# A tile's scatter stands two steps later in GpSimd's queue, in a four-layer graph attention kernel

## The chip, the cores and the metric

One Trainium2 chip, one core. The metric is the device time of one execution in microseconds (us).

## The reference

Four graph attention layers follow each other on 3327 nodes with 512 features, with 8, 4, 1 and 8 heads. Each layer normalizes, projects, scores every edge, takes a softmax over the neighbours and adds the weighted rows to `x`; layers 1 and 2 end in an ELU. Layer 0, with what all share:

```python
h = jnp.maximum(_layernorm(x, axis=-1), 0.0)
h = (h @ W.T).reshape(n, Hh, d)
e_src = jnp.einsum('nhd,hd->nh', h, a_src)
e_dst = jnp.einsum('nhd,hd->nh', h, a_dst)
e = jax.nn.leaky_relu(e_src[:, None, :] + e_dst[None, :, :], negative_slope=0.2)
mask = adj + jnp.eye(n, dtype=adj.dtype) > 0
e = jnp.where(mask[:, :, None], e, -jnp.inf)
alpha = jax.nn.softmax(e, axis=1)
out = jnp.einsum('ijh,jhd->ihd', alpha, h)
x = x + out.reshape(n, Hh * d)
```

The adjacency is sparse: a node has some 17 neighbours, itself included.

## The kernel before

A first part (to about 280 us of the profile) turns the rows of `adj` into neighbour lists and sorts the nodes by their degree into 26 tiles of 128. It also projects `x` for layer 0 into a table in DRAM, `tabx`. For layers 1 to 3 the tables are `tab`, two of them in turn. A row of a table has 528 numbers: the 512 projected features and the scores of the heads.

The second part, `tile_gat_lists`, runs the layers. Per layer it goes through the tiles from the one with the shortest lists to the one with the longest (11 to 36 slots, `CAPS`). The slots of a tile are cut into groups of four, and each group is a step, so that a tile takes 3 to 9 steps. A step of a group does this:

- `fetch`: GpSimd issues one indirect DMA per slot (L786), which gathers 128 rows of the table into a quarter of a buffer `g`. There are seven buffers `g` (`LOOK = 7`), and a step fetches the group that comes six steps later, so a fetch waits until VectorE has finished the group that used the buffer before.
- `scored`: VectorE adds the scores of source and target (`z`, L839, L841), ScalarE takes the exponential into `pw` (L842). It is done one step ahead of the products.
- `group`: with more than one head, VectorE multiplies the gathered rows by their weights into `m` (L865; three buffers), and TensorE adds the four products up in PSUM with matmuls by the identity (L870, tile `bank`). With one head VectorE does it alone (L860).

After a tile's last group at step `s` its end is spread over later steps: divisors and means on VectorE, the addition to `x` (`added`), and, except in the last layer, the next layer's normalization and projection: ScalarE subtracts the mean and squares (`xn` L915, `waste` L918), VectorE takes the root (`ve` L923 and on), TensorE transposes (`pt` L451), ScalarE applies the ReLU (`hT` L458), TensorE projects (`pv` L469), and ScalarE scales the result into the block of rows `v` (L476, three buffers). Then SP copies `v` to `own` (L941), and GpSimd scatters `v` into the next layer's table by an indirect DMA (L794), since the tiles are sorted and the table is not. In the last layer nothing is projected; the scatter there writes `x` to the output.

The order of the instructions is written out by hand: within the schedule TensorE, VectorE, ScalarE and GpSimd execute what is given to them in the order of the Python calls, whatever is ready. `later(s, place, piece)` puts a piece into step `s`; a step runs the fetch of the group six steps on, then the pieces at "first", the scores of the next group, the pieces at "scored", the products of this group, and the pieces at "last". A piece of one step on one engine thus stands in front of all pieces of later steps on that engine. `scatter` issues all scatters that wait at that moment. For a tile with more than one head `ends` is called with the step two after its last group.

Beside the lists, in layer 0 nine tiles of `adj` are gathered as masks (`Mask`), and in layers 1 to 3 the tiles with the longest lists (1, 9 and 2 of them) are computed densely with masks, in pieces between the same steps (`Several`, `Wholes`); these end through `ends` as well.

Of the kernel before, what the change touches and what calls it, by code (L numbers as in the profile page):

```python
# [22 lines left out]
HEADS = [8, 4, 1, 8]  # L23
# [724 lines left out]
def tile_gat_lists(ctx: ExitStack, tc: tile.TileContext, x, adj, ws, avs, out, ident, half, slots, L, low, spare, tabx, tabs):  # L748
# [48 lines left out]
    class Tile:  # L797
# [146 lines left out]
        def ends(self, s):  # L944

            b = s + 1 if ELU[self.l] else s
            for d, place, piece in [(s + 1, "scored", self.bent), (b, "last", self.added),
                                    (b + 1, "scored", self.centre), (b + 1, "last", self.root),
                                    (b + 2, "first", self.turn), (b + 2, "last", self.cut),
                                    (b + 3, "last", self.project), (b + 5 - (HEADS[self.l] == 1), "scored", self.rows),  # L950
                                    (b + 5, "last", scatter)]:
                later(d, place, piece)

        def finish(self, s):
# [319 lines left out]
    def later(s, place, piece):  # L1274
        at.setdefault((s, place), []).append(piece)
# [120 lines left out]
```

## Time and profile before

| what | us |
|---|---|
| median of three runs | 2964.49 |
| lowest, highest of them | 2949.65, 2972.24 |
| the profiled execution: time | 2978.08 |
| the profiled execution: span of its instructions | 2976.4 |
| first to last gather of layers 0, 1, 2, 3 in it (about) | 280 to 1072, 1112 to 1776, 1827 to 2275, 2318 to 2947 |
| busy: TensorE, VectorE, GpSimd, ScalarE | 2249.4, 1939.2, 1771.0, 890.3 |

The profile is of one execution. Engines are PE (TensorE), DVE (VectorE), ACT (ScalarE), POOL (GpSimd) and SP. A group's row gives the line, the engine, the operation, what is written and read, the count, then the busy time and the mean of one in ns, then the idle time of the engine just ahead of these instructions and what ended it. In a timeline each row has its start, its duration, and in brackets the idle time ahead of it and who ended it; "issue" is time in which the engine waited for nothing that the profile shows, "remote" a release whose origin it does not show.

### The profile page before, as it was taken

How to read it: one execution, taken by the hardware profiler on the slowest of the kernel's cores; microseconds unless marked ns; L12 is line 12 of the kernel's file. 1: busy time of each engine (PE TensorE's matmuls, PEld its weight loads, DVE VectorE, ACT ScalarE, POOL GpSimd, SP SyncE). 2: the span in 40 equal slices, each digit the busy share in tenths (PEclk: the TensorE clock that was granted, in tenths of full speed). 3: DMA queues.
4: the chain of work that ended last, by engine and by line, in shares of the span. 5: the costliest groups of instructions: out<-in, count | busy, mean ns of one | idle time of the engine just before them, and what ended most of it. 6: DMA issues, size and time to landing. Idle time of an engine off the chain costs nothing. (4 is left out here: it accounts for less than half of the span.)

```text
span 2976.4 us, 26618 instructions
## 1 busy us (share of the span) xinstructions
PE 2249.4 (76%) x6832; PEld 1233.1 (41%) x6832; DVE 1939.2 (65%) x5056; ACT 890.3 (30%) x2321; POOL 1771.0 (60%) x1774
## 2 busy tenths in 40 slices
PE   3777687777866775789787776768795588887877
PEld 2665243433433332445344433335454344444443
DVE  8897656645644545677566664787888366666656
ACT  4782122222211112333223222343333232323221
POOL 6993565655655636566566653565554566666664
PEclk9888888988988897999898988889798788888889
DMA  6784577776776657767676754777775666666664
GB/s 234 289 322 153 164 235 228 229 220 206 233 216 185 184 129 206 207 208 222 188 215 203 213 167 147 234 228 250 215 253 160 179 202 200 197 200 194 197 197 127
DMA packets 253306, 612.96 MB, mean 206 GB/s; under 512 B 90963, under 2 KB 108371, under 8 KB 248662
## 3 DMA queue, kind: packets, MB, share of 16 engines
q0 software_dynamic: 131120, 455.33, 51.6%
q1 hardware_dynamic: 118278, 149.01, 15.4%
q10 hardware_dynamic: 3744, 6.82, 0.7%
q8 instruction: 56, 0.92, 0.1%
q14 instruction: 108, 0.88, 0.1%
HBM read 544.13 MB, written 66.89 MB: 205 GB/s over the span
## 5 line engine op out<-in xcount | busy, mean ns | idle before, releaser
L870 PE MATMUL bank<-m,ident 128*128 128x512 f32 x2608 | 1320.9, 655 | 322.3 <-DVE m L865 189.4
L865 DVE TENSOR_TENSOR m<-g,pw 128x512 f32<-128x512 f32 x1304 | 810.9, 681 | 535.3 <-ACT pw L842 309.4
L870 PEld LDWEIGHTS bank<-m,ident 128*128 128x128 f32 x2608 | 525.9, 209 | 973.8 <-issue 631.1
L786 POOL DMA_INDIRECT g<-tab,idxb x734 | 701.7, 956 | 376.5 <-issue 199.8
L469 PE MATMUL pv<-w,hT 128*128 128x264 f32 x1664 | 450.7, 429 | 82.3 <-ACT hT L458 42.4
L469 PEld LDWEIGHTS pv<-w,hT 128*128 128x128 f32 x1664 | 349.9, 213 | 189.2 <-ACT hT L458 48.9
L786 POOL DMA_INDIRECT g<-tabx,twiceb x342 | 324.9, 950 | 148.6 <-issue 94.8
L786 POOL DMA_INDIRECT g<-tab,idxa x297 | 285.2, 960 | 159.6 <-issue 85.9
L842 ACT ACTIVATE pw<-z 128x32 f32<-128x32 f32 (+5 forms) x434 | 83.3, 192 | 878.1 <-DVE z L841 454.4
L1069 PE MATMUL whole<-ve,em 128*128 128x512 f32 x468 | 229.5, 639 | 52.5 <-DVE em L1055 17.3
L794 POOL DMA_INDIRECT tab<-v,idxb x54 | 54.1, 1002 | 243.6 <-ACT v L476 219.7
L630 POOL TENSOR_TENSOR key<-a,keys 128x3328 int32<-128x3328 int32 x26 | 189.4, 7293 | 4.2 <-DMA a<-in_adj 3.6
L860 DVE SCALAR_TENSOR_TENSOR bank<-g,pw,bank 128x512 f32<-128x512 f32 x243 | 183.2, 754 | 12.5 <-DVE bank L860 3.2
L1069 PEld LDWEIGHTS whole<-ve,em 128*128 128x128 f32 x468 | 92.0, 203 | 167.1 <-issue 114.3
L451 PE MATMUL pt<-ident,xn 128*128 128x128 f32 x416 | 70.8, 297 | 107.8 <-ACT xn L915 25.6
L637 DVE MAX8 cand<-key 128x8 f32<-128x208 int32 x416 | 143.6, 364 | 1.4 <-POOL key L630 1.4
L839 DVE TENSOR_TENSOR z<-g,pw 128x32 f32<-128x32 f32 (+5 forms) x434 | 74.3, 171 | 102.8 <-DMA g<-tab,idxa 63.0
L786 POOL DMA_INDIRECT g<-tabx,twicea x99 | 94.7, 957 | 74.9 <-issue 41.5
L458 ACT ACTIVATE hT<-pt 128x512 f32<-128x512 f32 x104 | 61.1, 588 | 200.0 <-remote 111.6
L476 ACT ACTIVATE v<-pv,rstd 128x528 f32<-128x528 f32 x78 | 54.2, 695 | 210.7 <-PE bank L870 104.5
L451 PEld LDWEIGHTS pt<-ident,xn 128*128 128x128 f32 x416 | 53.6, 151 | 150.7 <-issue 48.6
L1210 ACT ACTIVATE spare<-room,low 128x64 f32<-128x64 f32 x208 | 57.8, 336 | 183.8 <-remote 81.7
(173 smaller groups left out, 2216.1 us busy)
## 6 DMA issues: line engine op xcount, KB each, us to landing
a<-in_adj SPq DMA_DIRECT2D x26, 1664.0 KB
own<-v SPq DMA_DIRECT2D x78, 264.0 KB
ve<-tab SPq DMA_DIRECT2D x78, 264.0 KB
g<-own SPq DMA_DIRECT2D x66, 264.0 KB
tabx<-vx SPq DMA_DIRECT2D x26, 528.0 KB
g<-tab,idxb POOLq DMA_INDIRECT x734
low<-tab SPq DMA_DIRECT2D x52, 132.0 KB
room<-tab SPq DMA_DIRECT2D x52, 132.0 KB
```

Of the source, the lines that this page charges most:

```text
L451: nc.tensor.transpose(pt[:, k, :], xn[:, k * P:(k + 1) * P], ident)
L458: nc.scalar.activation(hT, pt, AF.Relu)
L469: nc.tensor.matmul(pv[:, s, :HF + 8], hT[:, k, :], W.w[:, k, s, :], start=(k == 0), stop=(k == KC - 1))
L630: nc.gpsimd.tensor_tensor(key, a, keys, OP.mult)
L637: nc.vector.max(cand[:, g * 8:(g + 1) * 8], key[:, g * SEG:(g + 1) * SEG])
L786: nc.gpsimd.indirect_dma_start(out=out_, out_offset=None, in_=table, in_offset=bass.IndirectOffsetOnAxis(ap=which, axis=0))
L839: nc.vector.tensor_tensor(z, g[:, :n, ROW - 8:ROW - 8 + H], self.s.unsqueeze(1).to_broadcast([P, n, H]), OP.add)
L842: nc.scalar.activation(self.wt[:, k0:k0 + n, :H], z, AF.Exp)
L860: nc.vector.scalar_tensor_tensor(acc, v, w, acc, OP.mult, OP.add)
L865: nc.vector.tensor_tensor(m[:, q, :].rearrange("p (s h d) -> p s h d", s=2, d=D), v.rearrange("p s (h d) -> p s h d", d=D), wt[:, k0 + q, ...
L870: nc.tensor.matmul(self.po, ident, m[:, q, :], start=(k0 + q == 0), stop=(k0 + q == K - 1))
L1069: nc.tensor.matmul(tl.po.rearrange("p (s m) -> p s m", s=2), e[:, q * P:(q + 1) * P], v.rearrange("p (s m) -> p s m", s=2)[:, :, :F // 2], ...
```

## The change

In `ends`, the scatter of a tile is put at the end of step `b + 7` where it was at the end of `b + 5`, where the layer has more than one head (layers 0, 1 and 3). `rows`, which makes `v`, stays in step `b + 5`. For one head (layer 2) the expression gives `b + 5` as before.

```diff
                                     (b + 3, "last", self.project), (b + 5 - (HEADS[self.l] == 1), "scored", self.rows),
-                                    (b + 5, "last", scatter)]:
+                                    (b + 7 - 2 * (HEADS[self.l] == 1), "last", scatter)]:
                 later(d, place, piece)
```

In GpSimd's queue the scatters of layers 0, 1 and 3 move behind the gathers of two further steps. The orders of the other engines and of SP are the same as before. In layer 0, for example, a scatter that stood between 12 and 8 gathers now follows the 8.

## Prediction

> **What bounds the kernel now.** I read the page first, then the busy times by layer, then who waits for whom in each layer, then the scatter's own line, and last the timelines of GpSimd, ScalarE and VectorE around single scatters.
>
> ```profile
> PE 2249.4 (76%) x6832; PEld 1233.1 (41%) x6832; DVE 1939.2 (65%) x5056; ACT 890.3 (30%) x2321; POOL 1771.0 (60%) x1774
> ...
> L786 POOL DMA_INDIRECT g<-tab,idxb x734 | 701.7, 956 | 376.5 <-issue 199.8
> ...
> L794 POOL DMA_INDIRECT tab<-v,idxb x54 | 54.1, 1002 | 243.6 <-ACT v L476 219.7
> ```
>
> No engine is full over the span. GpSimd's 60% is misleading: in a run of gathers each takes 0.95 us and 0.30 us of issue, so one starts every 1.254 us. The second and third lines are the gathers and the scatters; the scatter's idle column is what the change is about: GpSimd stood 219.7 us waiting for the row block `v` that ScalarE writes at L476 (the `idxb` tiles alone).
>
> By layer (windows from each layer's first gather to its last):
>
> ```profile
> 280.00:1072.00 792.00, 591.93 (x1653) 295.85 (x1652) 450.91 (x1207) 157.14 (x325) 473.47 (x497) 0.87 0.70 209
> 1112.00:1776.00 664.00, 521.86 (x1476) 273.87 (x1477) 421.63 (x1135) 190.87 (x590) 406.91 (x428) 0.89 0.70 205
> ...
> 2318.00:2947.00 629.00, 499.56 (x1607) 264.71 (x1608) 381.42 (x802) 180.17 (x628) 386.07 (x403) 0.85 0.68 197
> ```
>
> The columns are length, PE, PEld, DVE, ACT, POOL busy with counts, clock, DMA share, GB/s. With 0.3 us added to each, GpSimd's 428 instructions in layer 1 take 428 x 1.254 = 537 of 664 us, in layer 0 623 of 792, in layer 3 505 of 629. The rest is pauses. In all three layers the period of a tile is thus GpSimd's issue time plus its pauses; TensorE's busy time (522 in layer 1) is almost as long. So both are candidates for the bound, and the question is what ends a pause.
>
> Now the waits of GpSimd at the scatter (us, times), of VectorE for gathered rows (us, times, longest), both in the window of layer 1:
>
> ```profile
>   ACT v L476: 95.2, 21
> DVE z L839 <- DMA g<-tab,idxa: 24.3, 6, 17.0
> ```
>
> In layer 0 the first is 122.9 us in 20 waits. But the second line says that the gathers held up behind the scatter are not late: VectorE waits for rows six times in layer 1, all at its start. In the timelines the last gather of a group is issued 11 to 36 us before VectorE takes the group, in the body of either layer. So GpSimd's wait as such costs nobody a late row.
>
> The last view is one scatter of layer 1, in the timelines of GpSimd, ScalarE and VectorE:
>
> ```profile
> 1349.86 0.95 POOL L786 DMA_INDIRECT g<-tab,idxb  x1 [0.30 <-issue]
> 1353.65 0.70 ACT L476 ACTIVATE v<-pv,rstd 128x528 f32<-128x528 f32 x1 [6.49 <-PE bank L870]
> 1354.63 0.99 POOL L794 DMA_INDIRECT tab<-v,idxa  x1 [3.82 <-ACT v L476]
> 1355.75 0.15 DVE L923 TENSOR_SCALAR ve<-squares 128x1 f32<-128x1 f32 x1 [6.08 <-ACT waste L918]
> 1355.92 0.97 POOL L786 DMA_INDIRECT g<-tab,idxb  x1 [0.30 <-DVE ve L923]
> ```
>
> TensorE had issued the last of `pv`'s matmuls at 1346.83, yet ScalarE gets word only at 1353.65, 2.84 us after GpSimd's last gather ended (1350.81). The same in layer 0, with `hT` at the head of ScalarE's queue:
>
> ```profile
> 694.38 0.94 POOL L786 DMA_INDIRECT g<-tabx,twiceb  x1 [0.30 <-issue]
> 706.86 0.99 POOL L794 DMA_INDIRECT tab<-v,idxb  x1 [11.54 <-ACT v L476]
> ...
> 698.68 0.60 ACT L458 ACTIVATE hT<-pt 128x512 f32<-128x512 f32 x1 [16.37 <-remote]
> ```
>
> `hT`'s transposes started at 682.09 to 682.41; ScalarE sees them at 698.68, 3.36 us after the last gather's end (695.32). Wherever ScalarE stands for a result of TensorE that is long done, the wait ends 2 to 4 us into a pause of GpSimd. In layer 3, which has no `v`, the pauses come from full gather buffers, and they are longer:
>
> ```profile
> 2684.76 0.95 POOL L786 DMA_INDIRECT g<-tab,idxb  x1 [0.30 <-issue]
> 2692.81 0.95 POOL L786 DMA_INDIRECT g<-tab,idxb  x1 [7.09 <-DVE m L865]
> ```
>
> My reading, inferred from the timing and not shown by a cause in the trace: while gathers stream, TensorE's signals are held back, and a pause lets them through. The scatter's wait is then a valve: it stops the stream once per tile, just when ScalarE needs TensorE's word.
>
> **What the skill says.** "Trainium Architecture — The Big Picture", section "Inside one NeuronCore": every engine has its own instruction stream and meets the others only through semaphores. The trace agrees: gathers whose buffer is free stand behind a scatter that waits (1355.92 follows 1354.63). "Perfetto Trace Analysis", section "DMA Instruction — SWDGE (GPSIMD)": the profiled end of such a DMA is the end of descriptor generation, not of the data. Agrees: the first group of layer 1 is issued by 1115.25 and used at 1118.00, 2.75 us later. "DMA: Bandwidth & Descriptors", section "Anatomy of one DMA — SWDGE (gpsimd) path", gives 2.0 us plus bytes over 436e3; for 264 KB that is an estimate of 2.6 us, near that 2.75, and near the time into a pause at which the held signals arrive. No page says that gathers hold TensorE's signals back.
>
> **The change part by part.** Nothing is removed or added: 26 scatters in each of layers 0, 1 and 3 move two steps later, past the gathers of two steps (up to 8, so 10 us of issue). SP's copy of `v` (L941) stays where it is. Layer 2 has one head and is unchanged.
>
> Layer 3: its scatter waits for the finished `x`, and nearly always goes at once; its three longest waits sum to 24.5 us, and no gather behind it is needed within 11 us. 0 us, at most 24 gained if that is wrong.
>
> Buffers: `v` has three, a tile lasts about 27 us, so a buffer is asked for again some 80 us later; holding it 10 us longer costs 0. Without that cover ScalarE would wait up to 10 us a tile. Ends of layers: the last gathers have been issued before the last scatters, so nothing is passed: 0.
>
> Layers 0 and 1, the scatter passed by gathers. For each scatter I looked up when VectorE had freed the buffer that the next step's gathers need. In layer 1, 16 scatters that waited over 1 us had it free by the start of the pause (within 0.3 us); 55 gathers stand there. In layer 0 it is 11 scatters and 45 gathers. At these 27 GpSimd will go on instead of pausing: 100 gathers x 1.254 = 125 us of streaming before the valve opens, if signals come only in pauses. The buffer after that is typically free 9 us after the old pause began, and VectorE's way there leads through ScalarE's blocked `v`, so the pause comes anyway, later, and ends only when VectorE has finished another group. After the release in the example VectorE needs `ve`, the root (2 us), divisors, `z`, and four products (2.48 us), to 1361.70: 8 us, against the 1 us that the scatter needed.
>
> What a pause becomes: the 27 last 3.7 us on average now. Ended by a buffer, layer 3 shows what they last: 23 over 3 us sum to 132, so 5.7 us. Upper bound, with the longer way of layer 1: a delay of the whole 125 us, and 20 more for buffers that come free later. I take layer 3's value, measured, because some signals do pass during a stream: 27 x (5.7 - 3.7) = +54 us. At nine further scatters of layer 0 the buffer comes free only after the pause began; GpSimd then resumes at the buffer instead of at `v`; their sum is -9 us. Total +45 us. Lower bound: every wait at a scatter in layers 0 and 1 (218 us) is pure loss; see the rivals.
>
> **The sum.** The profiled execution spans 2976.4 and took 2978.1 us; +45 gives 3023. The median shown is 2964.5, 13.6 lower, so 3010 us there, 1.5% slower.
>
> **Rivals.**
> First, a wash: the rows are early, GpSimd's wait turns into a wait for buffers of the same length. For it: layer 3 without any such wait pauses about 5.2 us a tile, layer 1 4.9, layer 0 6.2. Layer 1 would gain 0.3 a tile, layer 0 lose 1.0: +7 - 25 = -18 us, about 2946, no measurable difference. Against it: the chain from ScalarE to the next free buffer is longer in layers 0 and 1 than in layer 3.
> Second, the other side: the blocked queue is the loss, as it looks. GpSimd issues for 537 of 664 us in layer 1; if its pauses there and in layer 0 (127 and 169 us) shrink by about a fifth, since a stream that starts earlier gives VectorE and TensorE deeper stock, the gain is 60 us: 2905. It decides if TensorE's signals are late for another reason than the stream (then the release does not wait for a pause, and a pause is only lost issue time). For it: GpSimd's issue time is the longest sum in layer 0. Against it: no row is late.
> Third, signals held throughout: +145 us, 3110, if nothing passes during a stream.
> That the change does nothing: no, the order in GpSimd's queue differs in layers 0, 1 and 3.
>
> **How the numbers follow.** Slower by the later valve 0.45, held throughout 0.10, wash 0.20, faster 0.25. A measurement of this kernel tells about 1% from no change. So slower 0.55, same 0.20, faster 0.25. The range 2900 to 3090 takes in the wash and the faster case at its value, and the slower case up to 125 us; beyond are the held-throughout case and larger gains. The likeliest case alone runs from 2985 to 3050.
>
> **What would show it.** Right: the wait of the scatter for `v` in layers 0 and 1 falls from 218 us to under 40; GpSimd's waits for VectorE's buffers rise by more than that; the waits of `hT` and `v` on TensorE grow; layer 2 keeps its length and layer 3 too; layers 0 and 1 together grow by some 45 us. Wrong: GpSimd's total pauses in these layers fall and ScalarE's waits on TensorE with them, or ScalarE's late wake-ups come in the midst of a stream of gathers.

## The result, and the profile after

The changed kernel takes 3085.03 us (median of 4 runs, 3078.26 to 3088.94), the kernel before, beside it, 2968.36 (2949.65 to 2985.0): a ratio of 1.0392, 95% interval 1.0326 to 1.0459. The forecast was 3010. The profiled execution of the changed kernel took 3086.79 us with a span of 3084.8, 108.4 more than before.

The same kernel before took 2511 to 2516 us in five of the eight groups of experiments and 3004 to 3009 in the other three, so there are two settings, called the prompt one and the late one here, and the measurement above belongs by its trace to the late one. Each experiment is compared with the kernel before of its own group.

The page of the changed kernel, rows as in the part on before, with ScalarE's row for `v` added (line, engine, operation, tiles, count; busy us and mean ns; idle ahead of it and what ended it), and below it that row of the kernel before:

```profile
PE 2269.4 (74%) x6832; PEld 1239.2 (40%) x6832; DVE 1940.1 (63%) x5056; ACT 891.4 (29%) x2321; POOL 1768.3 (57%) x1774
...
L786 POOL DMA_INDIRECT g<-tab,idxb x734 | 700.4, 954 | 498.7 <-issue 199.2
...
L476 ACT ACTIVATE v<-pv,rstd 128x528 f32<-128x528 f32 x78 | 54.2, 694 | 309.3 <-remote 119.8
...
L794 POOL DMA_INDIRECT tab<-v,idxb x54 | 54.1, 1001 | 158.4 <-ACT v L476 137.9
```

```profile
L476 ACT ACTIVATE v<-pv,rstd 128x528 f32<-128x528 f32 x78 | 54.2, 695 | 210.7 <-PE bank L870 104.5
```

No engine is busy much longer than before (TensorE by 20 us). GpSimd's wait at the scatter shrank (243.6 to 158.4 on this row), its wait at the gathers grew by more (376.5 to 498.7), and ScalarE's wait ahead of `v` grew from 210.7 to 309.3 us.

By layer, first gather to last (columns as before: length, PE, PEld, DVE, ACT, POOL busy, clock, DMA share, GB/s):

```profile
282.40:1099.60 817.20, 600.33 (x1649) 294.68 (x1649) 450.94 (x1204) 156.56 (x324) 475.62 (x500) 0.85 0.69 204
1144.30:1877.10 732.80, 535.56 (x1483) 280.25 (x1484) 420.75 (x1132) 191.97 (x590) 407.26 (x428) 0.85 0.64 185
...
2418.40:3055.90 637.50, 495.03 (x1603) 262.80 (x1603) 380.06 (x798) 179.98 (x627) 386.46 (x404) 0.85 0.68 194
```

Against 795.4, 663.7 and 629.1 in the same cut of before, layer 0 is 22 us longer, layer 1 69 and layer 3 8. Layer 2 has 449.8 against 447.2. The stretch ahead of the first gather (282.4 against 275.9) and the change from layer 0 to 1 (44.7 against 40.4) add 11; no moved scatter is in the first of these.

Layer 1 is where to look. GpSimd's waits there, at the scatter and for the buffers:

```profile
  ACT v L476: 42.5, 4
POOL g L786 <- DVE m L865: 128.6, 25, 11.7
```

The first stood at 95.2 us in 21 times; what is left of it is at the end of the layer. In the body no scatter waits over 0.3 us. The second was 42.8 in 21, 9.1 the longest. From GpSimd's timeline in this layer, stops of over 1.5 us between two instructions: before, 31 of them, 118.9 us, of which 19 at the scatter with 3.7 us in the mean; after, 29, 199.6 us, none at the scatter and nearly all for a buffer, and nine of them last over 10 us.

One of those nine, in the timelines of TensorE, GpSimd, ScalarE and VectorE:

```profile
1674.53 3.72 PE L469 MATMUL pv<-w,hT 128*128 128x264 f32 x16
1683.75 0.27 PE L1233 MATMUL whole<-low 128*128 128x129 f32 x1 [1.73 <-issue]
1685.84 0.59 PE L870 MATMUL bank<-m,ident 128*128 128x512 f32 x1 [1.82 <-issue]
1688.65 1.92 PE L870 MATMUL bank<-m,ident 128*128 128x512 f32 x2 [2.21 <-issue]
1687.19 0.95 POOL L786 DMA_INDIRECT g<-tab,idxb  x1 [0.30 <-issue]
1691.59 0.70 ACT L476 ACTIVATE v<-pv,rstd 128x528 f32<-128x528 f32 x1 [15.22 <-remote]
1692.81 0.63 ACT L895 ACTIVATE ex<-neg 128x512 f32<-128x512 f32 x1
1693.47 0.70 DVE L901 SCALAR_TENSOR_TENSOR bank<-ex,bank 128x512 f32<-128x512 f32 x1 [14.59 <-ACT ex L895]
1695.98 2.48 DVE L865 TENSOR_TENSOR m<-g,pw 128x512 f32<-128x512 f32 x4 [0.25 <-ACT pw L842]
1698.73 0.94 POOL L786 DMA_INDIRECT g<-tab,idxb  x1 [10.59 <-DVE m L865]
```

TensorE finished `pv` at 1678.25. GpSimd streams on to 1688.14, and ScalarE starts `v` at 1691.59, 13.3 us after the matmuls and 3.45 us into GpSimd's stop. Then the chain runs: `neg`, `ex`, `bank`, `x`, the scores, `pw`, four products to 1698.46, and only then is there a buffer for the gather. In the kernel before a stop at the scatter ends with `v`; this one lasts 6.4 us beyond the end of `v` (1692.29).

The trace also holds the times at which TensorE's signals reach the semaphore that counts them, which the views do not print. Between 1671.9 and 1688.2 us three arrive, though TensorE ends eleven matmuls there that send one; between 1691.57 and 1691.90 nine arrive. Signals that follow the one before within 0.06 us are 165 of the 410 recorded in layer 1 of the kernel before and 188 of 416 here, but none of 559 and none of 561 in layer 1 of two traces shown below, e6_before and e14_sp_rows_after. In layers 0, 1 and 3 every burst of four or more (75 in the kernel before, 75 here) falls between two indirect DMAs that stand over 1 us apart, 0.7 to 5.4 us after the end of the last one; none falls in a stream. So the held signals, which the prediction inferred, are in the record. And TensorE itself is held up: ahead of the matmuls at 1683.75, 1685.84 and 1688.65 it stands 5.8 us in all for nothing that the profile shows, though the last products to add up (`m`) were ready at 1678.88 and its clock was granted in full from 1678.3 to 1687.3 (1.00).

### The profile page after: what moved, and what is told of

It is laid out like the page before. It is cut to its first block, busy times and chain, and to the rows that moved or that the text cites. A ratio compares the mean times of both kernels' runs of the same rounds, so it can differ in the third digit from the quotient of the medians.

```text
span 3084.8 us, 26614 instructions
## 1 busy us (share of the span) xinstructions
PE 2269.4 (74%) x6832; PEld 1239.2 (40%) x6832; DVE 1940.1 (63%) x5056; ACT 891.4 (29%) x2321; POOL 1768.3 (57%) x1774
## 5 line engine op out<-in xcount | busy, mean ns | idle before, releaser
L870 PE MATMUL bank<-m,ident 128*128 128x512 f32 x2608 | 1344.5, 663 | 399.8 <-DVE m L865 258.8
L786 POOL DMA_INDIRECT g<-tab,idxb x734 | 700.4, 954 | 498.7 <-issue 199.2
L870 PEld LDWEIGHTS bank<-m,ident 128*128 128x128 f32 x2608 | 532.5, 212 | 1074.0 <-issue 647.4
L469 PE MATMUL pv<-w,hT 128*128 128x264 f32 x1664 | 441.9, 423 | 56.4 <-ACT hT L458 31.6
L794 POOL DMA_INDIRECT tab<-v,idxb x54 | 54.1, 1001 | 158.4 <-ACT v L476 137.9
L476 ACT ACTIVATE v<-pv,rstd 128x528 f32<-128x528 f32 x78 | 54.2, 694 | 309.3 <-remote 119.8
L923 DVE TENSOR_SCALAR ve<-squares 128x1 f32<-128x1 f32 x78 | 11.8, 151 | 152.9 <-ACT waste L918 136.3
```

Of the source, the lines that this page charges most:

```text
L469: nc.tensor.matmul(pv[:, s, :HF + 8], hT[:, k, :], W.w[:, k, s, :], start=(k == 0), stop=(k == KC - 1))
L786: nc.gpsimd.indirect_dma_start(out=out_, out_offset=None, in_=table, in_offset=bass.IndirectOffsetOnAxis(ap=which, axis=0))
L870: nc.tensor.matmul(self.po, ident, m[:, q, :], start=(k0 + q == 0), stop=(k0 + q == K - 1))
```

## The experiments

Lengths by layer below run from VectorE's first score (`z`) of the layer to its last product (`m`), which can be read in every kernel's trace in the same way. In the late setting, rows of different groups compare only roughly: the kernel before of the later groups (e12 to e14, e17, e18) is some 40 us slower than that of the first traces:

| kernel (setting) | layer 0 | layer 1 | layer 3 |
|---|---|---|---|
| before, first trace (late) | 773.9 | 684.0 | 642.4 |
| after, first trace (late) | 798.7 | 751.4 | 649.5 |
| e13_after (late) | 795.9 | 756.8 | 654.5 |
| e12_pause (late) | 777.6 | 711.4 | 653.8 |
| e18_valve (late) | 774.1 | 710.3 | 659.4 |
| e17_two_valves (late) | 771.8 | 703.2 | 655.0 |
| e14_sp_rows_after (late) | 798.7 | 532.1 | 661.1 |
| e6_before (prompt) | 626.8 | 540.4 | 508.7 |
| e5_after (prompt) | 622.9 | 542.4 | 510.8 |
| e10_sp_rows (prompt) | 626.3 | 532.2 | 510.8 |

### Parts of the change alone: e1_layer1, e2_layer0, e3_one_step

The theory: the stop at the scatter let TensorE's signals through, and without it they come later ("the valve"). Rivals: the later scatter costs something by itself; the blocked queue was a loss. These three make parts of the change.

```diff
-                                    (b + 5, "last", scatter)]:
+                                    (b + 5 + 2 * (self.l == 1), "last", scatter)]:   # e1_layer1
+                                    (b + 5 + 2 * (self.l == 0), "last", scatter)]:   # e2_layer0
+                                    (b + 6 - (HEADS[self.l] == 1), "last", scatter)]: # e3_one_step
```

> The scatter stands two steps later in layer 1 alone. Valve theory (a stream of gathers holds TensorE's signals back and the scatter's wait let them through): layer 1 carries most of the loss, its gathers take some 69 us longer than before (664 to 733), so about 2968 + 70 = 3038 us; the pauses of GpSimd in layer 1 are 10 to 12 us and end at a buffer, those of layer 0 stay as before. Rival (the loss is spread over the moved scatters alike, for instance by the output writes of layer 3 or the start of the next layer): a third of the loss, about 3007.

> The scatter stands two steps later in layer 0 alone. Valve theory: layer 0 has nine mask gathers and half of its pauses ended at a full buffer already, so it loses only some 25 to 35 us: 2993 to 3003. Rival (spread alike): 3007. With the run of layer 1 alone the two should add up to the loss of the whole change, 117, up to 10.

> The scatter stands one step later instead of two, in layers 0, 1 and 3. Valve theory: the stream runs on through the next step's gathers and then stops at a buffer that VectorE has not freed, so in layer 1 the scatter never stands ahead of the end of that pause; one step costs nearly all of it: 3060 to 3085 us. Rival (loss in proportion to the distance moved): half, about 3027.

Measured, with the kernel before at 2516.43 us: 2517.42 (1.0006, 0.9996 to 1.0017), 2513.34 (0.9993, 0.9981 to 1.0005) and 2517.54 (1.0009, 0.9997 to 1.002). No part costs anything, and the kernel before is 450 us faster than the one the prediction was made on. So these runs did not decide between the theories; they showed that the loss depends on something outside the kernel.

### The whole change, and the kernel before, in the prompt setting: e5_after, e6_before

> The changed kernel itself, beside the kernel before on one chip. The four experiments before this one ran where the kernel before took 2516 us and showed no late signal of TensorE. If the loss needs late signals (my theory), it depends on whether this chip shows them: with the kernel before near 2965 us, the ratio is 1.03 to 1.045; with it near 2516 us, the ratio is 1.00 (0.998 to 1.002), since each single part gave that. Rival (the parts add to more than their sum, whatever the chip): 1.01 or more also where the kernel before takes 2516 us.

> The kernel before, for its trace on the same chip. If it takes near 2516 us: no wait of ScalarE for TensorE ends 2 to 4 us into a pause of GpSimd, and VectorE waits for gathered rows over 100 us in all (against 44 us in layers 1 and 3 of the first trace); the first part up to the first gather takes the same 275 us as before, so that the whole difference of 450 us lies in the stages that gather. If near 2965 us: the same view as the first trace.

e5_after took 2514.53 us against 2513.04 (1.0, 0.9987 to 1.0014): no loss. The trace of e6_before (2516.81 us, one run) shows why. GpSimd in layers 0 and 1 of e6_before, its wait at the scatter, and VectorE's for rows (window from 360 to 1500 us), then one scatter in GpSimd's timeline, then layer 1 as a window:

```profile
POOL tab L794 <- ACT v L476: 26.5, 3, 25.7
DVE z L839 <- DMA g<-tabx,twiceb: 55.2, 30, 4.6
```

```profile
1187.21 0.95 POOL L786 DMA_INDIRECT g<-tab,idxb  x1 [0.30 <-issue]
1188.46 0.99 POOL L794 DMA_INDIRECT tab<-v,idxb  x1 [0.30 <-issue]
1189.76 0.97 POOL L786 DMA_INDIRECT g<-tab,idxb  x1 [0.31 <-DVE pw L837]
```

```profile
957.00:1494.30 537.30, 495.84 (x1535) 268.95 (x1536) 434.22 (x1161) 194.52 (x601) 407.22 (x428) 0.98 0.84 254
```

The 26.5 us are practically one wait at a layer's end; in the body nearly every scatter goes after the 0.3 us of issue, none after more than 1.3. GpSimd's 428 instructions of 1.254 us are 537 us, and layer 1 takes 537.3: the queue is never idle, so there is nothing that the place of a scatter could change. Rows are now what VectorE waits for. And the view has no wait for TensorE put down to `remote` any more, against 111.6 us for `hT` alone in the first trace. The first gather starts at 282.3 us, as in the late setting (275.9 and 282.4): the 450 us between the settings lie in the layers that gather.

### Late v by a fixed time, in the prompt setting: e8_late_before, e9_late_after

In this pair `v` is late in both, but by a time that no stop of GpSimd decides.

```diff
             if self.W is not None:
+                if HEADS[self.l] > 1:
+                    hold = work.tile([P, F], BF16, name="waste", bufs=1)
+                    for _ in range(20):
+                        nc.scalar.activation(hold, xs[self.t], AF.Copy)
                 v = scaled(nc, self.pv, self.rstd, work)
```

> The kernel before with ScalarE held for about 12 us per tile just ahead of v in layers 0 and 1 (20 copies of a row block into a scratch tile; output unchanged), so that v is late and the factors behind it too, as in the first trace, but by a fixed time that no pause of GpSimd decides. Expected on a chip without late TensorE signals: 2620 to 2820 us (VectorE's steps in layers 0 and 1 stand behind ScalarE by 2 to 6 us a tile, 52 tiles), GpSimd ahead of VectorE by several steps again and waiting for v at the scatter 2 to 8 us a tile.

> The same hold of ScalarE in the changed kernel; compared with e8_late_before. My theory (the loss needs signals that wait for a pause of GpSimd): GpSimd's waits for v turn into waits for VectorE's buffers, of 2 to 8 us more, and the time is that of e8_late_before within 0.4%. Rival A (a later and longer pause costs by itself, because rows or buffers come late after it): slower than e8_late_before by 2 to 4%. Rival B (the blocked queue is a loss, whatever makes v late): faster than e8_late_before by over 1%.

GpSimd's waits over the whole of e8_late_before, then of e9_late_after:

```profile
POOL tab L794 <- ACT v L476: 458.7, 49, 28.1
POOL g L786 <- DVE m L865: 45.3, 100, 3.9
```

```profile
POOL g L786 <- DVE m L865: 205.7, 91, 15.3
POOL tab L794 <- ACT v L476: 184.1, 30, 26.7
```

The waits move from the scatter to the buffers as in the changed kernel, with stops of up to 15.3 us. The times are 3025.02 and 3025.41 us against a kernel before of 2513.58: 1.2044 (1.2021 to 1.2068) and 1.2045 (1.2021 to 1.207). So in these two runs a late scatter, and a long stop that ends at a buffer, cost nothing by themselves, and a queue blocked at the scatter is no loss that moving it gets back. GpSimd has more slack here than in the late setting (537 us of issue in a layer 1 of 787 us from first gather to last, against 664), so for the late setting it is e18_valve, below, that settles whether the later scatter costs by itself. The size of the hold itself was misjudged: 20 copies of 0.631 us are 12.6 us a tile, and layers 0 and 1 grew by 496 us together, 9.5 a tile, where 2 to 6 were expected.

### Layer 1 without GpSimd's gathers: e10_sp_rows (prompt), e14_sp_rows_after (late)

SP copies rows of the same size; which neighbours' rows they are is left out in layer 1. e10 does it in the kernel before, e14 in the changed one.

```diff
+                elif l == 1:
+                    nc.sync.dma_start(g[:, q, :], tabs[1][t * P:(t + 1) * P, :])
```

> The kernel before, with layer 1's gathers replaced by plain copies of rows of the same size, issued by SP (it leaves out the choice of neighbours in layer 1: every slot of a tile gets that tile's own rows). GpSimd then only scatters in layer 1. On a chip without late signals, where layer 1 takes 537 us and GpSimd's 428 issues of 1.254 us are 537 us, I expect layer 1 to fall below 515 us (TensorE is busy for 496), the other layers to keep their lengths: so GpSimd's issue, not the scatter's place, would be what sets that layer. On a chip with late signals (kernel before near 2965 us) the stream theory expects layer 1 to fall from 664 to under 600 us and ScalarE's waits for long-done matmuls to vanish there alone; the rival, that the signals are late for a reason of TensorE's own, expects them to stay.

> The changed kernel with layer 1's gathers replaced by plain copies of rows, issued by SP (it leaves out the choice of neighbours in layer 1). With late signals (kernel before near 2965 us or more) the stream theory expects layer 1 to fall from 733 us to under 600 us, with next to no wait of ScalarE there that ends long after TensorE's work, while layers 0 and 3 keep theirs: 2900 to 2960 us. The rival (TensorE's signals are late whatever GpSimd does) expects layer 1 at 650 us or more. Without late signals: 2505 us, as the same exchange in the kernel before gave, since with an idle GpSimd the scatter's place can't matter.

e10 took 2505.27 us against 2515.24 (0.9952, 0.9938 to 0.9965). Layer 1 is 8 us shorter, where over 22 were expected: with GpSimd free, the layer stands at 532 us, where, as it reads, VectorE's chain holds it (438.6 us busy, and ScalarE's factors `pw` wait 290.2 us for its `z`).

e14 fell on the late setting: 2874.39 us against 3008.2 (0.9559, 0.949 to 0.9629). That is below the 2900 to 2960 that were expected. Windows in layers 0 and 1 of e14, and then ScalarE's waits for TensorE's work within layer 1:

```profile
280.00:1100.00 820.00, 592.47 (x1659) 292.36 (x1660) 455.04 (x1215) 158.28 (x328) 473.92 (x498) 0.86 0.69 203
1130.00:1680.00 550.00, 507.65 (x1582) 277.26 (x1582) 442.46 (x1188) 197.27 (x607) 24.09 (x25) 0.97 0.77 253
```

```profile
ACT hT L458 <- PE pt L451: 14.0, 11, 2.6
ACT v L476 <- PE pv L469: 7.9, 6, 1.7
```

Layer 1 drops from 756.8 us (e13_after, same group) to 532.1, the length that the same exchange has in the prompt setting (532.2), while layer 0, still gathered by GpSimd, keeps the 798.7 of the late one. In layer 1 no wait is put down to `remote` any more; in layer 0 of the same run `v` has 150.4 us of it in 10 times. The lateness comes with GpSimd's gathers and goes with them. With the issuer, the queue changes (110 MB move from the one that the page calls `software_dynamic` to `hardware_dynamic`), and so do the rows, one block in place of 128 found by index; which of the three it is stays open. The granted clock is no rival: it is 0.86 in layer 0 and 0.97 in layer 1 of this one execution, and e8_late_before has 0.86 over its whole length in the prompt setting, with none of the bursts.

### The change itself, and the stop put back, in the late setting: e13_after, e12_pause, e18_valve

```diff
+        def pause(self):                     # e12_pause, at (b + 5, "last")
+            if self.W is not None and HEADS[self.l] > 1:
+                for _ in range(4):
+                    nc.gpsimd.tensor_tensor(idle, idle, idle, OP.mult)
```

```diff
+        def valve(self):                     # e4, e7, e11, e16, e18: at (b + 5, "last"), self.block is v
+            if self.W is not None and HEADS[self.l] > 1:
+                nc.gpsimd.tensor_copy(small.tile([P, 1], F32, name="valve"), self.block[:, :1])
```

> The changed kernel itself, on another chip. With the kernel before near 2965 to 3010 us (late TensorE signals), my theory expects 1.03 to 1.045; with it near 2515 us, 0.998 to 1.002. The rival (the loss of the first measurement belonged to that one chip or session) expects no loss even where the kernel before is slow: below 1.012.

> The changed kernel with a pause of GpSimd of fixed length at the old place of the scatter, which waits for nothing: four products of a scratch tile (128x256 int32; an estimate of 0.6 us each from the 7.29 us of the 128x3328 one, and 0.3 us of issue, 3.4 us a tile, about the 3.7 us that GpSimd stood at the scatter in the first trace). On a chip with late TensorE signals (kernel before near 2965 us) the valve theory expects the loss gone or nearly (ratio 0.99 to 1.015), the rival 1.03 or more. On a chip without them, where GpSimd's queue is never idle in layers 0 and 1, 52 such pauses are 177 us of lost issue time, and nearly all of it shows: 2640 to 2700 us (1.05 to 1.075). If it costs much less there, GpSimd isn't the bound of these layers on such a chip.

> The changed kernel with GpSimd's one-column copy of v at the old place of the scatter. With late signals: 0.99 to 1.015 by the valve theory, 1.03 to 1.045 by the rival (the later scatter itself costs). Without late signals: 1.003 to 1.005, as measured.

e13_after took 3098.78 us against 3008.2: 1.032 (1.0252 to 1.0388). The loss is not one of the first measurement alone. ScalarE's row for `v` and GpSimd's for the gathers of e13_after:

```profile
L476 ACT ACTIVATE v<-pv,rstd 128x528 f32<-128x528 f32 x78 | 54.2, 695 | 330.6 <-remote 141.7 <-PE bank L870 99.1 <-PE pv L469 48.6
L786 POOL DMA_INDIRECT g<-tab,idxb x734 | 702.5, 957 | 510.5 <-issue 198.0 <-DVE m L865 160.1 <-DVE hv L435 43.0
```

e12_pause, in which GpSimd does 2.5 us of useless products at the scatter's old place and waits for nothing, took 3032.86 against 3009.29: 1.0094 (1.0068 to 1.012). Some seven tenths of e13_after's loss are gone, though GpSimd has more to do; in layer 1, 16 of the 27 bursts of TensorE's signals fall while these products run:

```profile
L949 POOL TENSOR_TENSOR idle<-idle 128x256 int32<-128x256 int32 x208 | 128.4, 618 | 13.5
```

e18_valve, in which GpSimd reads one column of `v` there, took 3021.18 against 3003.77: 1.0052 (1.0023 to 1.0081). Its scatter stays at `b + 7`. The waits within its layer 1 are those of the kernel before again, at another instruction:

```profile
POOL valve L947 <- ACT v L476: 77.7, 21, 5.6
POOL g L786 <- DVE m L865: 47.3, 18, 9.3
```

In the same cut of before (first score to last product) the scatter has 78.4 us in 20 times, and the gathers 42.8 in 21. So it is the stop that matters, not what GpSimd does after it.

### The same valve in the prompt setting: e4_valve, e7_valve, e11_valve, e16_valve

> The changed kernel, with one more GpSimd instruction at the end of step b + 5 in layers 0 and 1: a copy of one column of v, which must wait for v as the scatter did before; the scatter itself stays at b + 7. Valve theory: the wait does it, not the scatter's place: the pauses fall back to 3 to 5 us and the time to that of before, 2968, up to 10 more for the 78 us-free small instructions. Rival (it is the scatter's own writes or their place among the gathers that cost): stays at 3085.

> The changed kernel with a one-column copy of v on GpSimd where the scatter stood (end of step b+5, layers 0 and 1), the scatter staying at b+7. If this chip delays TensorE's signals (kernel before near 2965 us), the valve theory expects the time of before again (ratio 0.99 to 1.015), since GpSimd stands there until v is there; the rival, that the later scatter itself costs (its data are late for the next layer, or buffers are held), expects the loss to stay (1.03 to 1.045). If the chip doesn't delay them, 1.003 as on the first chip.

> The changed kernel with GpSimd's one-column copy of v at the old place of the scatter, once more, in case this chip delays TensorE's signals: with the kernel before near 2965 us the valve theory expects 0.99 to 1.015 of it, the rival 1.03 to 1.045. With the kernel before near 2516 us: 1.002 to 1.005, as twice before (two small instructions a tile in a queue that is never idle).

> The changed kernel with GpSimd's one-column copy of v at the old place of the scatter. With late signals the valve theory expects 0.99 to 1.015 of the kernel before, the rival (the later scatter itself costs) 1.03 to 1.045. Without late signals: 1.002 to 1.005, as before.

All four fell on the prompt setting: 1.0026 (1.0015 to 1.0038), 1.0037 (1.0015 to 1.0059), 1.0028 (1.0017 to 1.0039) and 1.0046 (1.0028 to 1.0064). The last three repeat the first in other groups. They give the price of the extra copies, 0.3 to 0.5%, which is also all that e18_valve loses: within the intervals its stop takes the whole loss away.

### One more stop a tile: e15_two_valves, e17_two_valves

The kernel before, and GpSimd reads one column of `hT` at the end of step `b + 2`.

```diff
+        def valve(self):                     # at (b + 2, "last"), after cut
+            if self.W is not None and HEADS[self.l] > 1:
+                nc.gpsimd.tensor_copy(small.tile([P, 1], F32, name="valve"), self.hT[:, 0, :1])
```

> The kernel before with one more pause a tile in layers 0 and 1: GpSimd copies one column of hT into a scratch tile at the end of step b+2, so it stands there until hT is there. With late signals (kernel before near 3000 us) the valve theory expects hT's waits (111.6 us in the first trace) to end sooner: 0.975 to 1.00. The rival, that any further stop of GpSimd only costs issue time, expects 1.005 or more. Without late signals (kernel before near 2515 us): 1.002 to 1.005, the price of two more instructions.

> The kernel before with one more pause a tile in layers 0 and 1, which ends when hT is there. With late signals (kernel before near 3000 us): 0.975 to 1.00 by the valve theory, 1.005 or more by the rival that a stop of GpSimd only costs issue time. Without late signals: 1.0016 as measured.

Prompt: 2515.3 against 2510.85 (1.0016, 1.0004 to 1.0029). Late: 3006.2 against 3003.77 (1.0, 0.9971 to 1.0029). In the late run, over layers 0 and 1:

```profile
POOL valve L936 <- ACT hT L458: 148.5, 33, 16.5
ACT hT L458 <- remote: 61.7, 8, 11.8
```

The late waits for `hT` fall from 111.6 us in the first trace to 61.7. GpSimd stands 148.5 us at the new instruction, but its waits at the scatter fall too, from 230.6 us in the same window of the first trace to 92.5, and the sum is nothing. This further stop is no better, and nothing tried here beats the kernel before in either setting, but for e10 and e14, which leave out part of the work.

## Why the prediction was right in direction and wrong in size

**The bound.** Right for the late setting in what it asked: what ends GpSimd's stops decides, and a row was never the trouble. That the issue time and the stops add up to the period is true of any engine and names no bound; e12 puts 128.4 us more work on GpSimd and is faster than the changed kernel. What the profile of one execution could not tell is that this is a setting: in the prompt one GpSimd has no stops over 1.5 us in layer 1 after its first gather.

**The mechanism.** Right, and now tested rather than inferred. TensorE's signals arrive in bursts, and only in GpSimd's stops; taking GpSimd's gathers out of a layer takes the late signals out of it (e14); a stop that waits for nothing gets most of the loss back (e12), one that waits for `v` all of it but its own price (e18); lateness that doesn't depend on a stop costs the moved scatter nothing (e8, e9). What in the chip holds the signals was not seen. In the late setting the record itself has gaps: 1706 of the 2108 signals that TensorE sends through this semaphore in the kernel before, where e6_before has them all. Whether the recording takes part in the lateness was not tested.

**The step that failed: the length of the stop after the change.** The prediction let the 27 stops grow from 3.7 to 5.7 us, with layer 3's stops as the measure, because some signals pass during a stream. For layer 1 that is 16 x 2.0 = 32 us, and the layer grew by 69. In the changed kernel the stops of layer 1 that end at a buffer and last over 3 us are 24 and sum to 187 us, so 7.8 us each: 16 x (7.8 - 3.7) = 66 us, nearly all of the 69. What was mis-sized is the part behind the signals. In 22 of these 24 stops a burst of TensorE's signals arrives, 2.5 us into the stop in the mean, and 5.6 us later the buffer is free; in layer 3 of the same trace the two parts are 3.0 and 3.0 us (18 stops). As the stop shown above reads, the difference is the way through the ELU: `v`, `neg`, `ex` and `bank` take 2.6 us from 1691.59 to the end of `bank` at 1694.17 before the next scores and products, and layer 3 has neither `v` nor an ELU. No run takes the ELU out. The prediction named "the longer way of layer 1" in its upper bound and then took the shorter one.

Its measure was also misread: three of layer 3's 23 stops are the scatter's own waits, two of them at the layer's end, and make 24.6 of the 132 us. The 20 others last 5.4 us, so by its own measure the forecast would have been lower still.

In layer 0, which has no ELU, the stops at a buffer over 3 us last 5.8 us, near the forecast. The sum there was 11 x 2.0 - 9 = +13 us and +22 was measured; what makes the other 9 stays open.

That the prediction's own bound for layer 1, 55 x 1.254 = 69.0 us, equals the measured 69 is not shown to be more than chance: it supposes that no signal passes during a stream, while some do (three in the stretch above), and in layer 0 the same bound, 45 x 1.254 = 56, was far off.

**Terms at nothing.** Layer 3 was priced at 0 and grew 8 us (7 in the other cut); the first stretch, the change of layer and layer 2 together add 13 more, less 4 at the later changes and the end. They stay unassigned: in the late traces below the table's first two rows layer 3 takes 653.8 to 661.1 us, also where its scatter was not moved (655.0 in e17_two_valves), so 8 us there are within what traces of this setting differ by. With layers 0 and 1 (91) they make the 108.

**Its own marks.** The wait for `v` in layers 0 and 1 was to fall from 218 to under 40 us: it fell to 110 (67.8 in layer 0, 42.5 in layer 1), since what stands at the ends of the layers stays, where the prediction had the moved scatter pass no gathers, and seven stops at `v` (33.2 us) were left in layer 0. GpSimd's waits for buffers did rise by more than the scatter's fell, `v`'s wait on TensorE did grow (`hT`'s fell, 111.6 to 61.0), and layer 2 kept its length. Of its signs of being wrong, late wake-ups in the midst of a stream, the bursts show none.

**The rivals.** Held throughout (3110, chance 0.10) came nearest in number, 25 us off, but by its reason, that nothing passes during a stream, that is luck. The wash (0.20) has its result in the prompt setting, where there is no wait at the scatter to turn into anything, and its very mechanism in e8 and e9: a wait at the scatter becomes an equal wait at a buffer. (In its working, layer 0's 169 us of pauses over 26 tiles are 6.5 us a tile, not 6.2.) The blocked queue as a loss (0.25) found support nowhere.

## What to carry to other kernels

An instruction that makes an engine wait can be useful through the wait itself: before a stall is moved out of a queue, ask what else gets done while the queue stands, and which wait takes its place and what chain ends that one. Price the new wait by the chain that releases it in the same layer, not by a like-looking stop in another. And run the kernel before beside every experiment: here its own time differed by a fifth from group to group, and the change was worth 3 to 4% in one setting and nothing in the other.

## What the runs showed of the hardware that was not expected

- The same program took 2511 to 2516 us in some groups of runs and 3004 to 3009 in others, steady within each group; whether this belongs to a chip or to a session was not settled. The record gives the same chip number, 0, for a group in each setting (2510.85 and 3003.77 us). The part ahead of the gathers has the same length in both (first gather at 271 to 282 us).
- In the late setting ScalarE learns of finished matmuls as much as 13 us late, as shown, while GpSimd issues indirect DMAs (0.95 us and 0.30 us of issue each), and about 3 us after it stops (2.84, 3.36 and 3.45 us in the three places shown). TensorE's signals then arrive in bursts, and TensorE itself stands for nothing that the profile shows (5.8 us in the stretch shown). In the prompt setting the same stream, without a stop in layer 1, holds nothing back.
- GpSimd's stop need not be idle: products on GpSimd (0.618 us each) got some seven tenths of the loss back, so it is the issue of gathers, their queue or their kind, not GpSimd's being busy, that goes with the late signals.
